# Level 3 cross attention of a Perceiver stack: divisions last, a longer pipeline, the norm in two parts, every second context early

## The chip, the cores and the metric

The kernel runs on one core of one Trainium2 chip. The metric is the device time of one execution in microseconds. The core has five engines with a queue each, and each works its queue strictly in order: PE multiplies matrices (its weight loads are listed as PEld), DVE works on vectors, ACT applies functions, POOL does elementwise work beside them, and SP issues transfers. They wait for each other by semaphores.

## The reference

A stack of four levels updates `x`, 64 batches of 32 rows of width 256. Each level has a cross attention to a context of 64 x 257 rows of width 256, a self attention and a feed-forward part. The change lies in the cross attention of level 3:

```python
qh = _split_heads(q @ Wq.T + bq)      # q = layernorm(x), 32 rows a batch, 16 heads of 16
kh = _split_heads(k @ Wk.T + bk)      # k = v = the batch's context, 257 rows
vh = _split_heads(v @ Wv.T + bv)
score = jnp.einsum('bhqd,bhkd->bhqk', qh, kh) / jnp.sqrt(jnp.float32(D_K))
attn = jax.nn.softmax(score, axis=-1)
out = jnp.einsum('bhqk,bhkd->bhqd', attn, vh)
...
return out @ Wo.T + bo                # added to x
```

Keys and values depend on the context alone, not on `x`, so they can be made at any time before they are needed.

## The kernel before

`x` stays in SBUF as 16 tiles of 128 rows, four batches to a tile (`NB` = 4). The cross attention of level 3 is `l3_xattn`. Its work is cut into steps for a batch b or a tile i:

- `loaded(b)` brings the keys and values of a context that was treated early (tile `kv`, 513 KB, from DRAM), or else its transposed context (tile `cT`, 257 KB).
- `keys_values(b)` does nothing for an early context; for another it makes keys (two halves, evicted by ACT) and values (evicted by DVE) with PE.
- `norm(i)` is the layer norm of a tile: statistics on DVE (L452, L454), the inverse root on POOL (`rsqrt`: L423 adds epsilon into `ln_r_v`, L425 raises it to -1/2 into `ln_r`), and the scaling on DVE (L458). `turned(i)` transposes it, `projected(i)` makes the queries and spreads them over heads (`qb`, POOL, L2713).
- `scores(b)` has PE fill four PSUM tiles `s`, of which there are just four; DVE takes each one's maximum (`nm`, L2788) and ACT its exponential (`e`, L2789) with the sums. The next batch's scores need the tiles back.
- `divided(b)`: DVE inverts the sums (`rs`, L2797), POOL multiplies `e` by them (L2798) and copies the last column (`pc`, L2799).
- `keys_first(b)` turns `e` on PE (L2807) and copies it out in two halves, `eT`, one by DVE (L2811), one by ACT (L2809).
- `weighted(b)` multiplies `eT` with the values; DVE picks each head's own part (`t`, L2825) and sums it into `oT` (L2831).
- `last_rows(i)` carries the weights of the 257th context row through DRAM (`ed`, `es`, SP's queue), and `output(i)` multiplies with the output weights and adds to `x`; POOL adds the bias to `x` (L2732), DVE the product (L2733).

A loop over n from -5 runs one step of each kind a turn, each with its own distance to n: `scores(n)`, `keys_values(n+1)`, `divided(n)`, `weighted(n-2)`, `keys_first(n-1)`; every fourth turn one each of the tile steps. The lists are below in the code and the diff. `as_written` chains the instructions of PE, DVE and ACT in the order in which the loop writes them. POOL's and SP's orders are left to a scheduler when the program is built; once built, they are fixed too.

The early contexts are made by `l3_keys_values`, 16 of them within the feed-forward part of level 0 and 16 within that of level 1, in pieces that `filled` puts between other work of PE there. Before, they are the contexts 0 to 31, so in the loop of `l3_xattn` the first 32 batches have no keys and values to make and the last 32 do.

Of the kernel before, what the change touches and what calls it, by code (L numbers as in the profile page):

```python
# [22 lines left out]
ALU = mybir.AluOpType  # L23
# [3 lines left out]
B, T, S, D = 64, 32, 257, 256  # L27
NT = B * T // 128
NB = 4
KP, KC = 96, 3  # L30
KL = S - 2 * KP
SP = KP * KC
# [2 lines left out]
LN_EPS = 1e-5  # L35
# [288 lines left out]
class Perceiver:  # L324
    def __init__(self, ctx, tc, a):
        self.tc, self.nc, self.a = tc, tc.nc, a
        nc = self.nc
        self.n_tiles = 0
        self.const = ctx.enter_context(tc.tile_pool(name="const", bufs=1))
        self.wpool = ctx.enter_context(tc.tile_pool(name="weights", bufs=N_SLOTS))  # L330
        self.x = self.sb(self.const, [128, NT, D], "x")
        self.cols = self.sb(self.const, [128, N_COL], "cols")
        self.con = self.sb(self.const, [128, N_CON], "con")
        nc.sync.dma_start(self.cols, a["cols"])
        self.ident = self.sb(self.const, [128, 128], "ident")
        make_identity(nc, self.ident)
        self.neg_half = self.sb(self.const, [128, 1], "neg_half")
        nc.gpsimd.memset(self.neg_half, -0.5)
        self.seed = self.sb(self.const, [128, 1], "seed", I32)
        nc.gpsimd.memset(self.seed, RSQRT_SEED + 1)  # L340

        self.ctx_st = self.sb(self.const, [128, 2 * B, 6], "ctx_st")
        self.ctx_st_x = self.sb(self.const, [B, 1, 6], "ctx_st_x")


        self.k_wT = self.sb(self.const, [128, 6, D], "k_wT")
        self.c_mean = self.sb(self.const, [128, B, 2], "c_mean")
        self.c_rc = self.sb(self.const, [128, B, 2], "c_rc")
        self.nxT = self.sb(self.const, [128, 2, B], "nxT")
        dram = ctx.enter_context(tc.tile_pool(name="rows_d", bufs=1, space=bass.MemoryType.DRAM))  # L350
        self.abd = self.sb(dram, [B, 2, S], "abd")

        self.kv = self.sb(dram, [B, 128, 2 * S + 2 * D], "kv")
        self.n_kv = 0

    def forms(self, pool):
# [667 lines left out]
        nc.vector.tensor_tensor(p, lg, bcast(ss, 2, 8), ALU.mult)  # L1024
        return p

    def l3_keys_values(self, one, ps, n):


        nc, a = self.nc, self.a  # L1030
        w = self.sb(one, [128, 2, 2, D], "kv_w")
        for j in range(2):
            nc.sync.dma_start(w[:, j], a["l3x_w"][1 + j].rearrange("p (k n) -> p k n", k=2))
        wk, wv = w[:, 0], w[:, 1]
        todo = range(self.n_kv, self.n_kv + n)
        self.n_kv += n
        ts = {}

        def loaded(b):
            if b in todo:  # L1040
                t = self.sb(self.wpool, [128, 2048], "w")
                nc.sync.dma_start(t[:, 0 : 2 * S], a["ctxT"][b])
                ts[b] = t

        def steps():
            for b in todo[:2]:
                loaded(b)
            for b in todo:
                loaded(b + 2)
                t = ts.pop(b)  # L1050
                cT = t[:, 0 : 2 * S].rearrange("p (k s) -> p k s", k=2)
                kv = t[:, 2 * S : 4 * S + 2 * D]
                for o in range(2):
                    pk = self.sb(ps, [128, S], "h")
                    self.mm(pk, [(wk[:, k, o * 128 : (o + 1) * 128], cT[:, k, :]) for k in range(2)])
                    nc.scalar.activation(
                        kv[:, o * S : (o + 1) * S], pk, AF.Identity, bias=self.col("L3_xattn_bk", o)
                    )
                    yield
                pv = self.sb(ps, [128, 2, D], "y")  # L1060
                for c in range(2):
                    self.mm(pv[:, c, :], [(cT[:, k, c * 128 : (c + 1) * 128], wv[:, k, :]) for k in range(2)])
                    if c == 0:
                        yield
                nc.scalar.copy(kv[:, 2 * S :], pv.rearrange("p c f -> p (c f)"))
                nc.scalar.dma_start(self.kv[b], kv)
                yield

        self.between = steps()

    def filled(self, n=1):
# [80 lines left out]
    def l0_ffn(self):  # L1152
        nc, tc, a = self.nc, self.tc, self.a
        wg = self.weight(a["l0f_wg"], 2)
        with ExitStack() as st:
            one = st.enter_context(tc.tile_pool(name="l0f_1", bufs=1))
            dram = st.enter_context(tc.tile_pool(name="l0f_d", bufs=1, space=bass.MemoryType.DRAM))
            ps = st.enter_context(tc.tile_pool(name="l0f_p", bufs=2, space=PSUM))
            tab = self.routing_tables(one)
            w = self.sb(one, [128, 8, 2048], "w_all")  # L1160
# [5 lines left out]
            rows = st.enter_context(tc.tile_pool(name="l2r", bufs=1))  # L1166
            one1 = st.enter_context(tc.tile_pool(name="l0s", bufs=1))
            pool = st.enter_context(tc.tile_pool(name="l0f", bufs=3))
            self.l3_keys_values(one1, ps, 16)
            p = self.probabilities(one, pool, ps, wg, None, nd)  # L1170
            st.enter_context(self.as_written(nc.vector))
            place = self.places(one, pool, ps, tab, p)
# [30 lines left out]
            at = self.sb(one, [128, NT, 8], "at")  # L1203
# [34 lines left out]
            for s in range(SLOTS):  # L1238
# [23 lines left out]
                y = self.sb(pool, [128, D], "y", bufs=2)  # L1262
# [372 lines left out]
    def l1_ffn(self, ahead, last):  # L1635
# [4 lines left out]
        with ExitStack() as st:  # L1640
# [11 lines left out]
            sums = self.sb(dram, [NT * 128, D], "sums")  # L1652
            nc.scalar.dma_start(sums.rearrange("(i p) f -> p i f", p=128), self.x)
            xn = self.sb(dram, [NT * 128, R], "xn")
            self.l3_keys_values(one, ps, 16)
            p = self.probabilities(one, pool, ps, wr, br, xn)
            nc.scalar.dma_start(xn.rearrange("(i p) f -> p i f", p=128)[:, :, D:R], p)
            place = self.places(one, pool, ps, tab, p)
# [982 lines left out]
    def l3_xattn(self):  # L2641
# [3 lines left out]
        with ExitStack() as st:  # L2645
# [44 lines left out]
                for hh in range(2):  # L2690
                    nc.sync.dma_start(nvd[:, hh::2, :], nv[hh * B : (hh + 1) * B])

            def norm(i):
                t_n[i] = self.normalized(pool, self.x[:, i, :], "n")

            def turned(i):
                pt = self.transposed(ps, t_n[i], "m")
# [48 lines left out]
                    )  # L2746

            def loaded(b):
                kv = self.sb(pool, [128, 2 * S + 2 * D], "kv", bufs=7)
                t_kv[b] = [kv[:, 0 : 2 * S].rearrange("p (k s) -> p k s", k=2), kv[:, 2 * S :].rearrange("p (c f) -> p c f", c=2)]  # L2750
                if b < self.n_kv:
                    nc.sync.dma_start(kv, self.kv[b])
                    return
                cT = self.sb(pool, [128, 2, S], "cT", bufs=4)
                nc.sync.dma_start(cT, a["ctxT"][b].rearrange("p (k s) -> p k s", k=2))
                t_c[b] = cT

            def keys_values(b):
                if b < self.n_kv:
                    return  # L2760
                cT = t_c[b]
                kT, v = t_kv[b]
                for o in range(2):
                    pk = self.sb(ps, [128, S], "m")
                    self.mm(pk, [(wk[:, k, o * 128 : (o + 1) * 128], cT[:, k, :]) for k in range(2)])
                    nc.scalar.activation(kT[:, o, :], pk, AF.Identity, bias=self.col("L3_xattn_bk", o))
                pv = self.sb(ps, [128, 2, D], "m")
                for c in range(2):
                    self.mm(pv[:, c, :], [(cT[:, k, c * 128 : (c + 1) * 128], wv[:, k, :]) for k in range(2)])
                nc.vector.tensor_copy(v, pv)  # L2770

            def scores(b):
                i, bl = b // NB, b % NB
                qb, kT = t_q[i][0], t_kv[b][0]

                pss = [self.sb(ps, [128, S], "s") for _ in range(4)]
                for c in range(2):
                    for r in range(4):
                        f = slice(32 * r, 32 * r + 32)
                        self.mm(  # L2780
                            pss[r][64 * c : 64 * c + 64],
                            [(qb[f, c, bl].rearrange("p h t -> p (h t)"), kT[f, c, :])],
                        )
                nm = self.sb(pool, [128, 4], "nm")
                e = self.sb(pool, [128, 4, S], "e")
                ss = self.sb(pool, [128, 4], "ss")
                for r in range(4):
                    nc.vector.tensor_reduce(nm[:, r : r + 1], pss[r], AX.X, ALU.max, negate=True)  # L2788
                    nc.scalar.activation(  # L2789
                        e[:, r, :], pss[r], AF.Exp, bias=nm[:, r : r + 1], accum_out=ss[:, r : r + 1]  # L2790
                    )
                t_e[b] = e, ss
# [40 lines left out]
                )  # L2833

            st.enter_context(self.as_written(nc.tensor, nc.vector, nc.scalar))
            for n in range(-5, B + 6):

                steps = [(loaded, n + 3, 1), (norm, n + 4, NB), (scores, n, 1), (keys_values, n + 1, 1)]
                steps += [(divided, n, 1), (turned, n + 3, NB), (projected, n + 2, NB)]
                steps += [(weighted, n - 2, 1), (keys_first, n - 1, 1), (last_rows, n - 4, NB), (output, n - 8, NB)]  # L2840
                if n == -4:
                    row_values()
                for step, at, per in steps:
                    if at % per == 0 and 0 <= at < B:
                        step(at // per)
# [95 lines left out]
```

## Time and profile before

Three runs took 3921.47, 3925.65 and 3926.65 us, median 3925.65. The profile is of another execution.

| | |
|---|---|
| profiled execution | 3939.03 us |
| its span | 3937.3 us |
| mean granted clock of TensorE | 0.955 |
| PE busy | 3546.4 us, 90% |
| PE's weight load busy | 2794.3 us, 71% |
| DVE busy | 1963.4 us, 50% |
| ACT busy | 1293.2 us, 33% |
| POOL busy | 1387.9 us, 35% |

The time of an engine is the sum over the whole program; the stages differ much, so a stage has to be read by itself. The granted clock is what the throttle let TensorE have, 1.00 being full speed. Where an engine was idle before an instruction, the profile names the instruction that ended the wait. Instructions are named by line, engine and operation, with the tile written and the tiles read, as `e<-s,nm`.

### The profile page before, as it was taken

To read this page: it belongs to the slowest core of one execution; us is meant where nothing else is said; L and a number is where in the kernel's file an instruction comes from. 1 tells how busy PE (TensorE), PEld (TensorE's weight loads), DVE (VectorE), ACT (ScalarE), POOL (GpSimd) and SP (SyncE) were. 2 spreads that over 40 slices of the span, in tenths; PEclk is the share of its full clock that TensorE was granted. 3 is DMA by queue.
4 is the path that set the end of the run, shared out by engine and by line. 5 is a ranking of instruction groups with operands and counts; after the bars stand their busy time and mean duration, and the time that the engine had idled before them with its cause. 6 is when DMAs were issued, how large, how long until landed. Compare 5 with 4: busy or idle time off the path is not lost.

```text
span 3937.3 us, 74907 instructions
## 1 busy us (share of the span) xinstructions
PE 3546.4 (90%) x29677; PEld 2794.3 (71%) x29677; DVE 1963.4 (50%) x5180; ACT 1293.2 (33%) x3551; POOL 1387.9 (35%) x1752
## 2 busy tenths in 40 slices
PE   7999778879899789799999899979999987998998
PEld 5788446756577667577777566669999965776776
DVE  5555665234344441677766466632222246554454
ACT  2333223423233132333333243322222235543332
POOL 5433751133311113555655244451121135333121
PEclk9999889989999889899999899999999989999999
DMA  6342007256100265333333000010000133110000
GB/s 211 124 153 87 8 7 257 89 188 208 50 2 2 80 184 166 107 91 84 86 85 93 25 1 2 23 66 1 1 1 1 44 102 101 37 42 22 7 7 12
DMA packets 176413, 281.11 MB, mean 71 GB/s; under 512 B 33536, under 2 KB 109824, under 8 KB 171840
## 3 DMA queue, kind: packets, MB, share of 16 engines
q1 hardware_dynamic: 155472, 239.58, 19.7%
q10 hardware_dynamic: 14976, 25.01, 1.8%
q0 software_dynamic: 5616, 11.74, 1.3%
q8 instruction: 236, 3.87, 0.4%
q14 instruction: 113, 0.93, 0.1%
HBM read 243.46 MB, written 32.79 MB: 70 GB/s over the span
## 4 chain that ended last, share of the span: by engine, by line
PE 72%; DVE 11%; POOL 6%; ACT 5%; issue 3%; DMA 2%; ACTq 0%; SPq 0%; DVEq 0%; POOLq 0%
PE m L471 32%; PE p L471 10%; PE s L471 5%; PE y L471 3%; PE h L471 3%; PE b L471 3%; PE o L471 3%; PE ab L471 2%; ACT e L2789 2%; DVE bd L970 2%; PE y L476 2%; PE k L471 1%; PE c L471 1%; POOL e L2798 1%; PE m L465 1%
## 5 line engine op out<-in xcount | busy, mean ns | idle before, releaser
L471 PE MATMUL m<-w,oT 128*128 128x256 f32 x1152 | 272.8, 387 | 23.4 <-ACT eT L2809 15.2
L471 PEld LDWEIGHTS m<-w,oT 128*128 128x128 f32 x1152 | 219.9, 194 | 63.1 <-ACT eT L2809 17.0
L471 PE MATMUL m<-nTg,w 128*128 128x256 f32 x1024 | 234.7, 387 | 4.3 <-ACT k L1520 2.9
L471 PEld LDWEIGHTS m<-nTg,w 128*128 128x128 f32 x1024 | 193.3, 192 | 35.6 <-ACT k L1520 4.9
L2798 POOL TENSOR_TENSOR e<-e,rs 128x1028 f32<-128x1028 f32 x64 | 121.7, 1902 | 200.2 <-DVE rs L2797 200.2
L471 PE MATMUL s<-cT,ut 128*128 128x257 f32 x768 | 181.1, 386 | 0.0
L471 PE MATMUL m<-pT,cn 128*128 128x384 f32 x512 | 176.2, 487 | 2.5 <-DVE pT L2174 2.5
L2151 ACT ACTIVATE p<-s,bi 128x257 f32<-128x257 f32 x192 | 88.9, 472 | 247.0 <-DVE bi L2147 226.7
L423 POOL TENSOR_SCALAR ln_r_v<-ln_mv 128x1 f32<-128x1 f32 x176 | 38.7, 223 | 348.1 <-DVE ln_mv L454 266.3
L471 PEld LDWEIGHTS s<-cT,ut 128*128 128x128 f32 x768 | 143.5, 193 | 19.4 <-ACT p L2151 0.2
L2789 ACT ACTIVATE e<-s,nm 128x257 f32<-128x257 f32 x256 | 118.1, 474 | 113.4 <-DVE nm L2788 93.1
L970 DVE STREAM_TRANSPOSE bd<-hs_p 32x512 f32<-32x512 f32 x192 | 134.8, 702 | 40.2 <-POOL hs_p L964 37.0
L2120 POOL TENSOR_TENSOR cT<-cT,ab 128x514 f32<-128x514 f32 x64 | 82.4, 1288 | 205.4 <-PE m L471 85.8
L471 PEld LDWEIGHTS m<-pT,cn 128*128 128x128 f32 x512 | 96.5, 189 | 58.7 <-DVE pT L2174 2.9
L2255 POOL TENSOR_TENSOR sr<-ss,neg_half 128x16 f32<-128x16 f32 (+1 forms) x33 | 95.0, 2879 | 113.1 <-DVE ss L2253 113.1
L471 PE MATMUL m<-w,nT 128*128 128x512 f32 (+2 forms) x320 | 126.2, 536 | 8.8 <-ACT nT L829 8.2
L2545 POOL TENSOR_TENSOR tB<-hB 128x512 f32<-128x512 f32 x8 | 10.2, 1271 | 326.2 <-ACT hB L2583 326.2
L471 PE MATMUL ab<-nTg,w 128*128 128x256 f32 x512 | 117.1, 388 | 6.5 <-DVE hA L2561 5.5
L471 PE MATMUL m<-w,nTg 128*128 128x512 f32 x256 | 117.7, 604 | 0.0
L471 PEld LDWEIGHTS ab<-nTg,w 128*128 128x128 f32 x512 | 98.2, 194 | 23.3 <-DVE hA L2561 9.2
L2160 POOL TENSOR_TENSOR p<-p,rs 128x771 f32<-128x771 f32 x64 | 95.2, 1488 | 46.7 <-DVE rs L2159 27.9
L471 PE MATMUL o<-bd,v 128*64 128x128 f32 (+1 forms) x1536 | 90.1, 287 | 21.4 <-DVE bd L970 21.4
(712 smaller groups left out, 8819.9 us busy)
## 6 DMA issues: line engine op xcount, KB each, us to landing
ct<-in_ctx SPq DMA_DIRECT2D x192, 256.0 KB
cT<-in_ctxT SPq DMA_DIRECT2D x32, 1028.0 KB
cT<-in_ctxT SPq DMA_DIRECT2D x96, 257.0 KB
ab<-abd SPq DMA_DIRECT2D x64, 257.0 KB
kv<-w ACTq DMA_DIRECT2D x32, 513.0 KB
kv<-kv SPq DMA_DIRECT2D x32, 513.0 KB
rb<-rd SPq DMA_DIRECT2D x16, 514.0 KB
w<-in_ctxT SPq DMA_DIRECT2D x32, 257.0 KB
```

Source lines behind the costliest of these rows:

```text
L423: nc.gpsimd.tensor_scalar(t, src, eps, None, ALU.add)
L465: self.nc.tensor.transpose(out[:, c, :], src[:, c * 128 : (c + 1) * 128], self.ident)
L471: self.nc.tensor.matmul(out, lhsT=l, rhs=r, start=j == 0, stop=j == last)
L476: self.nc.tensor.matmul(out[:, 0:n], lhsT=cT[0], rhs=self.k_qm[:, 0, 0:n], start=True, stop=False)
L970: self.nc.vector.transpose(bd[q, :, b, :], p[q])
L2120: nc.gpsimd.tensor_tensor(cT, cT, bcast(ab[:, 0, :], 1, 2), ALU.mult)
L2151: nc.scalar.activation(p[:, g, :], pss[g], AF.Exp, bias=bi[:, g : g + 1], accum_out=ss[:, g : g + 1])
L2160: nc.gpsimd.tensor_tensor(p, p, bcast(rs, 2, S), ALU.mult)
L2255: nc.gpsimd.tensor_tensor(r, ss, self.neg_half[:p].to_broadcast([p, nh]), ALU.pow)
L2545: nc.gpsimd.tensor_tensor(t1, b12, b11, ALU.subtract)
L2789: nc.scalar.activation(e[:, r, :], pss[r], AF.Exp, bias=nm[:, r : r + 1], accum_out=ss[:, r : r + 1])
L2798: nc.gpsimd.tensor_tensor(e, e, bcast(rs, 2, S), ALU.mult)
```

## The change

- `divided(n)`, so far behind the keys and values in a turn, comes after `weighted`, `keys_first` and the first part of the norm. `weighted` works on n-3 instead of n-2 and `keys_first` on n-2 instead of n-1; `last_rows` and `output` follow one turn later. There are four tiles `e` instead of three and eight tiles `kv` instead of seven.
- `norm` is cut into `norm_1` (statistics and POOL's inverse root) and `norm_2` (the scaling), a turn apart. The order of a turn begins with `norm_2`, ahead of `scores`; `norm_1` stands ahead of `divided`.
- The early contexts are every second one, 1, 3, ... 63 (`early`), instead of 0 to 31. The PSUM tiles of `l3_keys_values` come from a function that is passed in, with 512 columns each.

```diff
+EARLY = 32
...
+        self.early = [b for b in range(B) if (b + 1) * EARLY // B > b * EARLY // B]
...
-    def l3_keys_values(self, one, ps, n):
+    def l3_keys_values(self, one, n, bank, buf=None):
...
-        todo = range(self.n_kv, self.n_kv + n)
+        todo = self.early[self.n_kv : self.n_kv + n]
...
-                    pk = self.sb(ps, [128, S], "h")
+                    pk = bank(o)[:, 0:S]
...
-                pv = self.sb(ps, [128, 2, D], "y")
+                pv = bank(2)
...
-            self.l3_keys_values(one1, ps, 16)
+            self.l3_keys_values(one1, 16, lambda j: self.sb(ps, [128, 512], "hhy"[j]))
...
-            self.l3_keys_values(one, ps, 16)
+            self.l3_keys_values(one, 16, lambda j: self.sb(ps, [128, 512], "hhy"[j]))
...
-            def norm(i):
-                t_n[i] = self.normalized(pool, self.x[:, i, :], "n")
+            def norm_1(i):
+                st = self.sb(pool, [128, 6], "ln_st")
+                nc.vector.bn_stats(st, self.x[:, i, :])
+                mv = self.sb(pool, [128, 2], "ln_mv")
+                nc.vector.bn_aggr(mv, st)
+                t_n[i] = mv, self.rsqrt(pool, mv[:, 1:2], LN_EPS, "ln_r")
+
+            def norm_2(i):
+                mv, r = t_n[i]
+                t_n[i] = self.sb(pool, [128, D], "n")
+                nc.vector.tensor_scalar(t_n[i], self.x[:, i, :], mv[:, 0:1], r, ALU.subtract, ALU.mult)
...
-                kv = self.sb(pool, [128, 2 * S + 2 * D], "kv", bufs=7)
+                kv = self.sb(pool, [128, 2 * S + 2 * D], "kv", bufs=8)
...
-                if b < self.n_kv:
+                if b in self.early:
...
-                e = self.sb(pool, [128, 4, S], "e")
+                e = self.sb(pool, [128, 4, S], "e", bufs=4)
...
-            for n in range(-5, B + 6):
-
-                steps = [(loaded, n + 3, 1), (norm, n + 4, NB), (scores, n, 1), (keys_values, n + 1, 1)]
-                steps += [(divided, n, 1), (turned, n + 3, NB), (projected, n + 2, NB)]
-                steps += [(weighted, n - 2, 1), (keys_first, n - 1, 1), (last_rows, n - 4, NB), (output, n - 8, NB)]
+            for n in range(-6, B + 8):
+
+                steps = [(loaded, n + 3, 1), (norm_2, n + 4, NB), (scores, n, 1), (keys_values, n + 1, 1)]
+                steps += [(turned, n + 3, NB), (projected, n + 2, NB), (weighted, n - 3, 1)]
+                steps += [(keys_first, n - 2, 1), (norm_1, n + 5, NB), (divided, n, 1), (last_rows, n - 5, NB), (output, n - 9, NB)]
```

More of the change, by code (lines that the diff above doesn't have):

```diff
@@ L1039, in loaded @@
         def loaded(b):
[L1040 to L1043, printed above, removed]
+            t = buf() if buf else self.sb(self.wpool, [128, 2048], "w")
+            nc.sync.dma_start(t[:, 0 : 2 * S], a["ctxT"][b])
+            ts[b] = t
         def steps():
@@ L1047, in steps @@
                 loaded(b)
-            for b in todo:
-                loaded(b + 2)
+            for at, b in enumerate(todo):
+                for c in todo[at + 2 : at + 3]:
+                    loaded(c)
                 t = ts.pop(b)
@@ L1059, in steps @@
                     yield
-                pv = self.sb(ps, [128, 2, D], "y")
+                pv = bank(2)
                 for c in range(2):
-                    self.mm(pv[:, c, :], [(cT[:, k, c * 128 : (c + 1) * 128], wv[:, k, :]) for k in range(2)])
+                    self.mm(
+                        pv[:, c * D : (c + 1) * D],
+                        [(cT[:, k, c * 128 : (c + 1) * 128], wv[:, k, :]) for k in range(2)],
+                    )
                     if c == 0:
                         yield
-                nc.scalar.copy(kv[:, 2 * S :], pv.rearrange("p c f -> p (c f)"))
+                nc.scalar.copy(kv[:, 2 * S :], pv)
                 nc.scalar.dma_start(self.kv[b], kv)
@@ L2758, in keys_values @@
             def keys_values(b):
-                if b < self.n_kv:
+                if b in self.early:
                     return
```

## The prediction

> **What bounds the kernel now.** I read the share of busy time by engine first (PE 90%), then stretches of the cross attention of level 3, which runs from the end of the first scores (3201.4 us) to the last output (3593.15 us), 391.7 us. Columns: stretch and its length, busy time of PE, PE's weight load, DVE, ACT and POOL with counts, granted TensorE clock, DMA share, GB/s.
>
> ```profile
> 3201.40:3370.00 168.60, 134.89 (x1438) 96.61 (x1442) 109.79 (x292) 88.98 (x332) 89.55 (x106) 0.93 0.31 95
> 3370.00:3593.20 223.20, 218.35 (x1892) 172.07 (x1886) 130.93 (x315) 108.86 (x369) 81.48 (x94) 1.00 0.14 40
> ```
>
> The first stretch holds the contexts whose keys and values were made early: PE idles there and the clock is 0.93. The second makes keys and values itself and PE is full. So interleaving the two kinds can fill the idle time, if the order of the waits allows it. The timeline of PE in the second stretch gives each piece of work at full clock (start, duration, instruction):
>
> ```profile
> 3454.55 0.69 PE L471 MATMUL s<-kv,qb 32*64 32x257 f32 x16
> 3455.16 2.00 PE L471 MATMUL m<-cT,w 128*128 128x257 f32 x8
> 3457.01 1.89 PE L471 MATMUL m<-w,cT 128*128 128x256 f32 x8
> ...
> 3459.04 1.14 PE L471 MATMUL m<-eT,kv 128*64 128x128 f32 x16
> 3460.12 1.09 PE L2807 MATMUL m<-ident,e 128*128 128x128 f32 x8
> ```
>
> From start to start: scores 0.62, keys and values 3.63, weighting 1.07, turning of e 1.02; once in four steps also 0.31 (turned), 0.98 (projected) and 1.49 (last rows and output). Four steps without keys and values are 4x2.71 + 2.79 = 13.63 us of PE, with them 28.15 (measured 28.24, so nothing is lost there). The early groups of four begin their outputs at 3242.01, 3263.15, 3284.36, 3304.05, 3325.31 and 3345.01: 20.60 each, 6.97 lost. All PE work is 64x2.71 + 32x3.63 + 16x2.79 = 334.2; the stage loses 57.5: 8 early groups 55.8, 8 late ones 0.7, edges 1.0.
>
> Where an early group loses it: DVE's, POOL's and PE's timelines over the same few microseconds (in brackets: idle time before, and what ended it).
>
> ```profile
> 3298.50 0.68 DVE L2811 COPY eT<-m 128x512 f32<-128x512 f32 x1
> 3299.09 0.42 DVE L452 BATCH_NORM_STATS2 ln_st<-x 128x6 f32<-128x256 f32 x1
> 3299.55 0.18 DVE L454 BATCH_NORM_AGGREGATE ln_mv<-ln_st 128x2 f32<-128x6 f32 x1
> 3300.74 0.41 DVE L458 TENSOR_SCALAR n<-x,ln_mv,ln_r 128x256 f32<-128x256 f32 x1 [1.02 <-POOL ln_r L425]
> ```
>
> ```profile
> 3297.72 1.90 POOL L2798 TENSOR_TENSOR e<-e,rs 128x1028 f32<-128x1028 f32 x1 [1.03 <-DVE rs L2797]
> 3299.68 0.19 POOL L2799 COPY pc<-e 128x4 f32<-128x4 f32 x1
> 3299.84 0.22 POOL L423 TENSOR_SCALAR ln_r_v<-ln_mv 128x1 f32<-128x1 f32 x1
> 3300.14 0.57 POOL L425 TENSOR_TENSOR ln_r<-ln_r_v,neg_half 128x1 f32<-128x1 f32 x1
> ```
>
> ```profile
> 3300.31 1.09 PE L2807 MATMUL m<-ident,e 128*128 128x128 f32 x8
> 3301.24 0.27 PE L2738 MATMUL m<-ident,pc 128*16 128x128 f32 x1
> 3304.05 2.07 PE L471 MATMUL m<-w,oT 128*128 128x256 f32 x4 [2.54 <-ACT eT L2809]
> 3305.92 1.06 PE L471 MATMUL m<-nvs,es 128*128 128x256 f32 x2
> ```
>
> DVE waits 1.02 for the norm's root from POOL, its queue stands, and PE idles 2.54. Then PE's work takes twice its time (2.07 against 1.03 in the late half). Stretches of 1 us of PE (busy, count, clock, DMA share, GB/s) say why:
>
> ```profile
> 3304.00:3305.00 1.00, 0.95 (x2) 0.50 0.01 3
> 3305.00:3306.00 1.00, 1.00 (x4) 0.50 0.02 5
> 3306.00:3307.00 1.00, 1.00 (x11) 0.50 0.00 0
> ```
>
> The clock is halved for about 3.4 us. Of the five such gaps listed, three were followed by this (groups of 21.14, 21.21, 21.26 us), two not (19.69, 19.70): 1.5 us each time.
>
> **The change, part by part.** *Every second context early.* As many contexts, matmuls, evictions and loads as before, here and in the two earlier stages that make them; PSUM tiles of 512 columns take the turns of those of 257 and 2x256. Cost there 0. Here odd steps n now do keys and values (of the even context n+1), even steps do not. A group of four needs 13.63 + 2x3.63 = 20.89 of PE.
>
> *Loads.* A pair brings 513 + 257 KB in some 13 us, 59 GB/s, against 95 carried in the first stretch without PE once waiting for a kv load. SP's queue holds the last rows' ed and es issues (four es take 1.7 us) ahead of loads needed about five steps, over 25 us, later; 0.
>
> *Divisions last, turning and weighting a step later.* DVE no longer stands for the exponentials (rs waits 1.1 us in each early step): t, oT and the copy eT come first, and rs finds its sums ready. The fourth e tile and eighth kv tile cover the extra step. On POOL the two qb (0.56 each) now stand ahead of the division of step 2 mod 4, and x + bo (0.72, after norm_2) ahead of that of step 0; a division is needed by PE two steps later, over 10 us, so 0. This gain is inside the PE-bound sum.
>
> *The norm in two parts.* This decides. norm_1 (statistics) stands on DVE at the end of a step n = 3 mod 4, ahead of rs; norm_2 stands first in the next step, ahead of the maxima nm. The built order of POOL in the changed kernel is ln_r_v, then e (the division of that step), then ln_r, then pc. So ln_r stands behind 1.90 us of division, DVE's queue behind norm_2, the exponentials behind nm, and the next scores behind the exponentials, which hold the four s banks. And the step is even: no keys and values cover it.
>
> I work it out from durations above, t = 0 at the start of scores(3). PE: scores to 0.62, keys and values to 4.25, weighting to 5.32, turning to 6.34, scores(4) to 6.96. DVE: t and oT 5.37 to 6.35, eT to 6.95, statistics to 7.5, rs to 7.7. POOL: ln_r_v at 7.7, e 7.9 to 9.8, ln_r to 10.35. DVE: norm_2 10.4 to 10.7, then nm at 0.33 each; the first exponential starts 0.53 after the first nm (11.25), they follow at 0.45; a bank is free 0.47 + 0.14 later (at the stage's start PE restarted 0.14 after an exponential): 11.85 for the first, 13.2 for the fourth, so scores(5) end at 13.6. Meanwhile weighting starts 0.15 late, as eT's two copies are not done, and turning ends at 9.2; without the wait scores(5) would end at 9.8. The group loses 3.80 + 0.15 = 3.95. The other three steps lose nothing: odd ones have keys and values, step 2 mod 4 has projected (0.98) on top of 2.09, against some 2.5 for nm and exponentials.
>
> That happens at n = 0, 4, ... 56: 15x3.95 = 59.3. Step 60 has no norm; its chain of nm and exponentials alone loses 0.85. Edges 1.0 as before. At the start the first norm's statistics run ahead of the row values while DVE waits for a DMA, which takes about 1.7 off, and keys and values of context 0 come in (3.63, partly under the 1.2 of qb): first scores end 0.6 earlier (bounds -0.8 and, at half clock, +3). Loss after: 59.3 + 0.85 + 1.0 - 0.6 = 60.5, against 57.5: +3.0 us before the clock is counted.
>
> *The clock.* The new gap is 9.2 to 11.85, 2.65 us, and then 1.4 us of scores that trickle in as banks come free. No row shows this very gap. Nearest: the 2.54 us gap, which halved the clock in 3 of 5 groups. Lower bound c = 0, as in the other two. Upper bound 3.3: at the stage's start the clock read 0.50 from 3198.25 to 3211.5, four spells in a row, with PE working between gaps; two spells cost 3.3. I take one spell in every group, since the low stretch is 4 us instead of 2.54: half of 3.4 us with keys and values queued behind, 1.7. 15x1.7 = 25.5.
>
> [...]
>
> Sum: +3.0 + 25.5 = +28.5. The profiled execution took 3939.03 (span 3937.3), 13.4 above the median of the three runs, 3925.65; on its span I expect 3966, on the median 3954. The runs spread over 5 us; 0.2% (7.9 us) is about what can be told from no change.
>
> **Rivals.**
> *Faster: the root comes in time.* If ln_r did not stand behind the division, or DVE reached norm_2 late, only the chain of nm and exponentials would be left, 0.85 a group: 15x0.85 + 0.85 + 1.0 - 0.6 = 14.0 of loss, -43.5, 3882. For it: PE has 57.5 to give and no other engine is above 66% in either stretch. Against it: POOL's and DVE's orders as built. With the clock staying full it decides from a loss of 3.75 a group; with c = 1.7, from 2.05.
>
> *The clock stays full.* c = 0 to 0.3: +3 to +7.5, 3929 to 3933. For it: two of five gaps. Against it: the trickle, which leaves PE nearly idle for longer.
>
> *Two spells a group.* c = 2.5 to 3.3: +40 to +52, 3966 to 3978. For it: the start of the stage, where sparse work did not bring the clock back; against it: in the groups of before one spell was always enough.
>
> *The gain does not appear because loads are late*: a kv load 3 us late in each group would add 45. I see nothing for it and fold it into the case above.
>
> **How the numbers follow.** Forecast (c 0.4 to 2.4: 3935 to 3965) 0.58; clock full 0.13; two spells 0.13; root in time 0.16. Predicted 3954. The range leaves out the last rival and the far end: from 3922 (+3 less an error of 0.4 a group) to 3975. Faster by over 0.2%: 0.16 less a little, 0.15. Within 0.2%: most of the full clock, 0.10. Slower: 0.75.
>
> **What would show it.** Right: DVE's n waits about 2.7 us for ln_r in 15 places, POOL shows e between ln_r_v and ln_r, ACT's exponentials wait for nm at every fourth step, PE idles 2.6 us there with 0.50 clock after it, groups of 26 to 27 us; rs no longer waits for exponentials. Wrong: n hardly waits, groups near 22, or the clock at 1.00 throughout the stage and groups near 24.8.

## The result, and the profile after

| | before | after |
|---|---|---|
| median of the runs | 3926.15 us (3921.47 to 3931.77, 4 runs) | 3970.55 us (3966.25 to 3971.83, 4 runs) |
| profiled execution, its span | 3939.03, 3937.3 | 3966.25, 3964.5 |
| cross attention of level 3, first scores' end to last output's end | 391.7 | 427.3 (3193.96 to 3621.25) |
| PE work of that stage at full clock | 334.2 | 334.2 |
| a group of four batches | 20.60 early, 28.24 late | 24.9 to 27.5 |

The change makes the kernel slower: ratio 1.0104, 95% interval 1.0089 to 1.0119. Groups are measured here between PE's starts of the projection of one tile and the next.

The stage grew by 35.6 us. The two halves no longer differ, and the clock is 0.91 in both. Stretches of the stage, columns as in the prediction (busy time of PE, PE's weight load, DVE, ACT and POOL with counts, granted clock, DMA share, GB/s):

```profile
3194.00:3400.00 206.00, 184.64 (x1566) 137.14 (x1568) 113.18 (x291) 98.84 (x348) 85.36 (x102) 0.91 0.23 68
3400.00:3621.30 221.30, 197.75 (x1741) 147.86 (x1738) 126.29 (x320) 100.60 (x351) 88.38 (x105) 0.91 0.19 57
```

The place itself, a turn n = 0 mod 4, in the timelines of DVE, POOL and PE (start, duration, instruction, idle time before and what ended it):

```profile
3402.59 0.18 DVE L2704 BATCH_NORM_AGGREGATE ln_mv<-ln_st 128x2 f32<-128x6 f32 x1
3402.69 0.16 DVE L2813 RECIPROCAL rs<-ss 128x4 f32<-128x4 f32 x1
3405.51 0.41 DVE L2710 TENSOR_SCALAR n<-x,ln_mv,ln_r 128x256 f32<-128x256 f32 x1 [2.66 <-POOL ln_r L428]
3405.84 1.41 DVE L2804 TENSOR_REDUCE nm<-s 128x1 f32<-128x257 f32 x4
```

```profile
3402.86 0.22 POOL L426 TENSOR_SCALAR ln_r_v<-ln_mv 128x1 f32<-128x1 f32 x1 [4.63 <-DVE rs L2813]
3403.05 1.90 POOL L2814 TENSOR_TENSOR e<-e,rs 128x1028 f32<-128x1028 f32 x1
3404.90 0.57 POOL L428 TENSOR_TENSOR ln_r<-ln_r_v,neg_half 128x1 f32<-128x1 f32 x1
```

```profile
3403.35 1.09 PE L2823 MATMUL m<-ident,e 128*128 128x128 f32 x8
3406.97 2.52 PE L474 MATMUL s<-kv,qb 32*64 32x257 f32 x16 [2.52 <-ACT e L2805]
3409.41 3.80 PE L474 MATMUL m<-cT,w 128*128 128x257 f32 x8
```

POOL has both values it needs at 3402.9. It takes the division `e` between the two halves of the root, so `ln_r` starts 2.04 us after `ln_r_v` instead of 0.3. DVE stands 2.66 us in front of `n` with four maxima behind it, and PE idles 2.52 us until the first exponential frees a bank. Then the next keys take 3.80 us where a matmul group of that kind took 2.00 in the late half before. Single microseconds of PE over the same place (busy, count, clock, DMA share, GB/s):

```profile
3406.00:3407.00 1.00, 0.03 (x1) 0.67 0.00 0
3407.00:3408.00 1.00, 1.00 (x5) 0.50 0.00 0
...
3412.00:3413.00 1.00, 1.00 (x3) 0.50 0.00 0
3413.00:3414.00 1.00, 1.00 (x6) 0.91 0.06 16
```

The clock is halved from 3406.35 to 3413.2: 6.8 us, twice the spell of about 3.4 that the kernel before showed. Over the whole stage, the waits of DVE and of PE (total us, times, longest):

```profile
DVE n L2710 <- POOL ln_r L428: 38.2, 15, 2.7
...
DVE rs L2813 <- ACT e L2805: 1.3, 2, 1.0
```

```profile
PE s L474 <- ACT e L2805: 38.3, 15, 3.1
```

The wait that the change was to remove is gone: `rs` waited 35.0 us in 32 places for the exponentials before, 1.3 now. In its place `n` waits 38.2 in 15 places (14.1 in 14 before), and PE's wait for the exponentials is of the same size and number. In 14 of the 15 places `n` waits 2.66 us behind the division. The first, at the stage's start, is another case: no division stands there yet, `n` waits 1.00 for the root alone, and PE's 3.06 are the length of the chain from the norm's statistics to the first exponential.

### The profile page after: what moved, and what is told of

It reads as the page before. It is cut to its first block, busy times and chain, and to the rows that moved or that the text cites. A ratio compares the mean times of both kernels' runs of the same rounds, so it can differ in the third digit from the quotient of the medians.

```text
span 3964.5 us, 74957 instructions
## 1 busy us (share of the span) xinstructions
PE 3571.5 (90%) x29677; PEld 2807.0 (71%) x29677; DVE 1962.4 (50%) x5180; ACT 1295.6 (33%) x3551; POOL 1386.9 (35%) x1752
## 3 DMA queue, kind: packets, MB, share of 16 engines
q1 hardware_dynamic: 155472, 239.58, 19.6%
## 4 chain that ended last, share of the span: by engine, by line
PE 73%; DVE 11%; POOL 5%; issue 4%; ACT 4%; DMA 3%; ACTq 0%; SPq 0%; DVEq 0%; POOLq 0%
PE m L474 33%; PE p L474 10%; PE s L474 6%; PE b L474 3%; PE y L474 3%; PE o L474 3%; PE h L474 3%; PE ab L474 2%; PE y L479 1%; DVE bd L973 1%; PE c L474 1%; PE k L474 1%; PE m L468 1%; PE m L2823 1%; PE y L480 1%
```

## The experiments

Theory: the built order of POOL, division ahead of `ln_r`, costs 3.95 us a group in a turn that no keys and values cover, and the clock falls in that gap. Rivals: the norm being in two parts is itself the trouble; the place of `norm_2` on DVE is; the clock is a minor part; interleaving the early contexts costs by itself (PSUM turns, loads). Each kernel was timed against the kernel before. Its stage and its group come from its profiled execution:

| kernel | median us | ratio [95%] | stage us | group us |
|---|---|---|---|---|
| before | 3926 to 3930 | | 391.7 | 20.6 early, 28.24 late |
| after | 3970.55 | 1.0104 [1.0089, 1.0119] | 427.3 | 27.31, at first 24.9 to 26.7 |
| norm_1 ahead of the division | 3895.51 | 0.9918 [0.9901, 0.9934] | 351.1 | 21.71 |
| norm whole again | 3976.05 | 1.0117 [1.0101, 1.0134] | 427.5 | 27.31 |
| norm_2 behind the maxima | 3902.66 | 0.9936 [0.9919, 0.9952] | 360.8 | 22.56 |
| the gap filled with matmuls | 3949.23 | 1.0057 [1.004, 1.0075] | 404.2 | 25.55 |
| even contexts early | 3918.15 | 0.997 [0.9958, 0.9982] | 379.4 | 23.61 |
| contexts 0 to 31 early | 3941.85 | 1.0032 [1.0019, 1.0044] | 408.6 | 19.6 to 20.6, then 29.95 to 31.7 |
| before, contexts interleaved | 3930.04 | 0.9999 [0.9988, 1.0009] | 385.7 | 23.88 |
| norm_1 ahead, output a turn earlier | 3879.65 | 0.9868 [0.9845, 0.9891] | 340.5 | 21.07 |

**The statistics moved ahead of the division.** The step `norm_1` is issued behind the maxima of the same turn, so that POOL meets the root before the division:

```diff
-steps = [(loaded, n + 3, 1), (norm_2, n + 4, NB), (scores, n, 1), (keys_values, n + 1, 1)]
+steps = [(loaded, n + 3, 1), (norm_2, n + 4, NB), (scores, n, 1), (norm_1, n + 5, NB), (keys_values, n + 1, 1)]
...
-steps += [(keys_first, n - 2, 1), (norm_1, n + 5, NB), (divided, n, 1), (last_rows, n - 5, NB), (output, n - 9, NB)]
+steps += [(keys_first, n - 2, 1), (divided, n, 1), (last_rows, n - 5, NB), (output, n - 9, NB)]
```

> The changed kernel with norm_1 moved up in the turn, right behind scores, and nothing else; in the built order of POOL ln_r then stands ahead of the division instead of behind it. Theory (the root stands behind 1.90 us of division, and DVE's queue with it): n no longer waits, the maxima start about 3 us earlier in 15 turns, scores end 0.65 late instead of 3.8, the clock stays full: groups of four near 21.7 us instead of 27.2, about 82 us less, near 3889. Rival (the longer pipeline, the later divisions or the interleaving cost the time, the norm's place is incidental): 3960 or more.

Measured: 3895.51 us, stage 351.1, group 21.71. POOL's and DVE's timelines of this kernel at the same turn:

```profile
3402.47 0.22 POOL L426 TENSOR_SCALAR ln_r_v<-ln_mv 128x1 f32<-128x1 f32 x1
3402.77 0.57 POOL L428 TENSOR_TENSOR ln_r<-ln_r_v,neg_half 128x1 f32<-128x1 f32 x1
3406.66 1.98 POOL L2814 TENSOR_TENSOR e<-e,rs 128x1028 f32<-128x1028 f32 x1 [3.32 <-DVE rs L2813]
```

```profile
3406.41 0.17 DVE L2813 RECIPROCAL rs<-ss 128x4 f32<-128x4 f32 x1
3406.49 0.39 DVE L2710 TENSOR_SCALAR n<-x,ln_mv,ln_r 128x256 f32<-128x256 f32 x1
```

The root is done 3.1 us before DVE reaches `n`, which has no wait any more, although the division is still issued at the same place. The stage falls by 76.2 us. This kernel holds everything else of the change, interleaving, longer pipeline, two-part norm, so that the place of `norm_1` alone turns a slower kernel into a faster one. The edit brings the statistics forward on DVE as well as the root on POOL; what the order on POOL does with the statistics left where they were, no run shows by itself.

**The norm in one piece again**, at the first place of the turn:

```diff
+def norm(i):
+    norm_1(i)
+    norm_2(i)
...
-steps = [(loaded, n + 3, 1), (norm_2, n + 4, NB), ...
+steps = [(loaded, n + 3, 1), (norm, n + 4, NB), ...
-steps += [(keys_first, n - 2, 1), (norm_1, n + 5, NB), (divided, n, 1), ...
+steps += [(keys_first, n - 2, 1), (divided, n, 1), ...
```

> The changed kernel with the norm in one part again at the head of the turn, as in the kernel before; divisions stay last, so in POOL's built order the division still stands ahead of the root. Theory (what costs is the division ahead of the root, not the cut in two): n still waits over 2 us, the maxima start only 0.35 us earlier; 5 us less, with the clock perhaps up to 20 less: 3950 to 3966. Rival (the cut of the norm costs the time): n waits 1.0 us as in the kernel before, 50 us or more less, 3920 or below.

Measured: 3976.05 us, stage 427.5, group 27.31. POOL's and DVE's timelines of this kernel:

```profile
3409.97 1.90 POOL L2818 TENSOR_TENSOR e<-e,rs 128x1028 f32<-128x1028 f32 x1 [4.16 <-DVE rs L2817]
3411.84 0.22 POOL L426 TENSOR_SCALAR ln_r_v<-ln_mv 128x1 f32<-128x1 f32 x1
...
3412.15 0.57 POOL L428 TENSOR_TENSOR ln_r<-ln_r_v,neg_half 128x1 f32<-128x1 f32 x1
```

```profile
3412.75 0.41 DVE L2714 TENSOR_SCALAR n<-x,ln_mv,ln_r 128x256 f32<-128x256 f32 x1 [2.33 <-POOL ln_r L428]
```

The cut of the norm is not the cause. Whole, the norm has both halves of the root behind the division, and DVE stands 2.33 us instead of 2.66. PE's gap is 2.18 instead of 2.52, and 13 of these 14 gaps were followed by two spells of half clock. That the wait is slightly shorter brought nothing: both kernels come out with groups of 27.31. The expectation, 3950 to 3966, missed. That the clock took back what the shorter wait gave is read from the equal groups, not tested.

**norm_2 behind the maxima**, with `norm_1` where the change put it:

```diff
-steps = [(loaded, n + 3, 1), (norm_2, n + 4, NB), (scores, n, 1), (keys_values, n + 1, 1)]
+steps = [(loaded, n + 3, 1), (scores, n, 1), (norm_2, n + 4, NB), (keys_values, n + 1, 1)]
```

> The changed kernel with norm_2 one place later in the turn, behind scores, so that DVE takes the maxima first; POOL's order stays (division ahead of the root). Theory (the wait is costly only because the maxima are queued behind it): n still waits, 1 to 2 us in 15 places, but exponentials and scores go on; about 80 us less, 3887 to 3897. Rival (a late root is costly wherever it stands): less than 20 us gained, 3950 or more.

Measured: 3902.66 us, stage 360.8, group 22.56. DVE's waits of this kernel:

```profile
DVE n L2710 <- POOL ln_r L428: 18.9, 14, 1.4
```

DVE still waits behind the division, for 1.4 us in 14 places, but the maxima have gone ahead and PE's next scores don't depend on the wait. The time fell by 68 us of the 75 that the first experiment gave, somewhat less than expected. So most of what the wait costs is set by what is queued behind it on DVE.

**The gap filled.** The after kernel, with matmuls on constant operands put at the end of each turn n = 0 to 56, n = 0 mod 4, where PE would idle. They go into a PSUM tile of which only one column is read, by a copy of ACT:

```diff
+def filler(n):
+    if n < 0 or n > 56:
+        return
+    pf = self.sb(ps, [128, 2, 128], "m")
+    for j in range(10):
+        self.mm(pf[:, j % 2, :], [(wq[:, k, 0:128], wq[:, k, 128:256]) for k in range(2)])
+    f = self.sb(pool, [128, 1], "filler")
+    nc.scalar.copy(f, pf[:, 1, 0:1])
...
+                if n % NB == 0:
+                    filler(n)
```

> The changed kernel with 20 extra matmuls of 128x128x128 (about 2.5 us of PE) at the end of every fourth turn, in the place of PE's gap; their result is thrown away (one column copied by ACT). The wait itself stays. Theory (half clock after the gap costs 1.7 to 3.4 us in each of 15 groups): the clock stays at 1.00, groups fall from 27.2 to 24.9, 30 to 36 us less, 3935 to 3941. Rival (the clock is incidental, all of the loss is the wait): no change, 3970, or more if the extra matmuls cost time.

Measured: 3949.23 us, stage 404.2, group 25.55. A long stretch and PE's timeline of this kernel:

```profile
3200.00:3400.00 200.00, 199.12 (x1955) 162.82 (x1955) 116.86 (x297) 98.59 (x353) 85.68 (x104) 1.00 0.23 65
```

```profile
3410.52 4.63 PE L474 MATMUL m<-w 128*128 128x128 f32 x40
3415.08 0.69 PE L474 MATMUL s<-kv,qb 32*64 32x257 f32 x16
```

The clock is 1.00 throughout, and the stage is 23.1 us shorter with 68 us more of PE work in it. The filler was mis-sized: 20 matmuls came out as 40 records and 4.63 us, not the 2.5 that I meant. The scores behind it start 4.56 us after the filler's start, where gap and trickle of the after kernel are 2.52 and 2.04 - 0.62 = 1.42, together 3.94; so it overshoots by about 0.6 in each of 15 groups, 9 us. The clock's part of the loss is then about 23.1 + 9 = 32 us, as an estimate. That is nearly all of the 35.6 by which the stage grew. It holds for the profiled execution, which was the fastest of the four (3937.34; the others 3945 to 3954); between the medians of the two kernels the gain is 21.3.

**The even contexts early** instead of the odd ones, everything else as in the after kernel. The wait stays and its turn now has keys and values:

```diff
-self.early = [b for b in range(B) if (b + 1) * EARLY // B > b * EARLY // B]
+self.early = list(range(0, B, 2))
```

> The changed kernel with the even contexts early (0, 2, ... 62) instead of the odd ones, and nothing else. The order of POOL stays (division ahead of the root), but the turn in which norm_2 waits now has keys and values to make, and the uncovered turn before it has none. Theory (the wait costs what no matmul work covers): n waits as long as in the changed kernel, but PE stands only about 1.45 us there (until the keys' eviction, which ACT does after the exponentials) and 0.85 in the turn before; groups near 23.3 us, no half clock; 60 us less than the changed kernel, 3905 to 3920. Rival (the wait is a fixed price wherever it falls): 3960 or more.

Measured: 3918.15 us, stage 379.4, group 23.61. DVE's and PE's waits in this kernel:

```profile
DVE n L2710 <- POOL ln_r L428: 38.4, 15, 2.7
```

```profile
PE m L2823 <- ACT kv L2782: 22.7, 14, 1.6
```

DVE's wait is as before the edit, 38.4 us in 15 places, and the kernel is 52 us faster. What remains is a smaller gap of 1.6 us: the eviction of keys stands behind the late exponentials on ACT, and PE's turning has to wait for it. After these gaps the clock stayed at 1.00. Here the parity of the early contexts alone decides whether the wait is covered.

**The first 32 contexts early**, as before the change, with the rest of the change:

```diff
-self.early = [b for b in range(B) if (b + 1) * EARLY // B > b * EARLY // B]
+self.early = list(range(EARLY))
```

> The changed kernel with the contexts 0 to 31 early, as in the kernel before: the new order without the interleaving. Theory: in the first half every turn is uncovered, groups stay near 20 us (norm's wait and half clock in place of the old waits); in the second half keys and values cover all but 1.5 to 2 us of the wait, groups 30 instead of 28.24: 3930 to 3950, between the kernel before and the changed one. Rival (the new order alone is the loss, the interleaving does not matter): 3965 or more.

Measured: 3941.85 us, stage 408.6. The early half of the stage takes 19.6 to 20.6 a group, the late half 29.95 to 31.7 against 28.24 of pure PE work. In the early half the wait of `n` lies uncovered and the clock falls at each of its seven gaps (2.09 to 2.52 us), as in the after kernel, though without keys and values the group is short. In the late half keys and values cover the wait itself, but seven gaps of 1.88 us before PE's turning stay, as in the experiment before, on top of 28.24 of PE work; four of them were followed by a half clock of some 3.4 us. Against the after kernel this is 29 us less: with half of the waits covered and half not, the kernel lies between the two.

**The kernel before, with the odd contexts early and nothing else** (the loop that loads ahead in `l3_keys_values` is fitted to a list; the PSUM tiles stay as before):

```diff
+self.early = list(range(1, B, 2))
...
-todo = range(self.n_kv, self.n_kv + n)
+todo = self.early[self.n_kv : self.n_kv + n]
...
-if b < self.n_kv:
+if b in self.early:
```

> The kernel before with every second context early and nothing else. Theory: without the later divisions an uncovered turn still takes some 4.1 us of DVE and ACT (the chain of maxima, exponentials, inverse sums, t, oT, eT in the profile of before) against 2.71 of PE, and the norm's turn 6 to 7: groups of 23.6 to 25 us, against 24.4 on the mean of the kernel before, so 3915 to 3945, little changed. Rival (interleaving by itself fills PE): 3890 or below.

Measured: 3930.04 us, stage 385.7, group 23.88. DVE's waits of this kernel:

```profile
DVE rs L2798 <- ACT e L2790: 35.7, 33, 1.2
```

Interleaving by itself changes nothing that can be told in the median (0.9988 to 1.0009) and takes 6 us off the stage. The wait of `rs` for the exponentials is untouched by it. So the loads of the interleaved contexts cost nothing that shows. The PSUM tiles of 512 columns are not in this kernel, but the profiles bear on them: the time outside the stage is 3545.5 and 3549.1 us in the two kernels with the old tiles and 3531.3 to 3548.0 in the eight with the new ones, so no cost of theirs stands out of that spread. Interleaving without the rest of the change does not bring the gain; which part of the rest it needs was not separated.

PE idles here too, 13 times for 2.52 to 2.53 us ahead of the output, and only the first of these gaps was followed by a half clock. The last section comes back to this.

**The first experiment, with the output a turn earlier.** Of its group of 21.71 PE's own work is 20.89. The output is issued in turn n = 1 mod 4, a turn that has keys and values as well; this edit puts it in the turn before, which has none:

```diff
-steps += [(keys_first, n - 2, 1), (divided, n, 1), (last_rows, n - 5, NB), (output, n - 9, NB)]
+steps += [(keys_first, n - 2, 1), (divided, n, 1), (last_rows, n - 5, NB), (output, n - 8, NB)]
```

> The changed kernel with norm_1 right behind scores and output one turn earlier (n - 8), so that its 1.49 us of PE stand in the turn n = 0 mod 4, whose matmuls are too short for the chain of maxima and exponentials. Theory: the last 0.8 us of a group (21.71 against 20.89 of PE) falls to 0.1 or 0.2: 9 to 10 us less than with norm_1 moved alone, about 3886. Rival (what is left of the 0.8 is not that chain): no change, 3895.

Measured: 3879.65 us, stage 340.5, group 21.07. The stage fell by 10.6 us, as expected, and the median by 15.9. The two profiled executions differ by 11.05 (3891.95 and 3880.90), nearly all of it the stage; where the rest of the difference of the medians lies is open. A stretch of this kernel:

```profile
3197.20:3400.00 202.80, 200.55 (x1969) 154.26 (x1970) 141.68 (x366) 122.27 (x435) 107.38 (x127) 1.00 0.29 86
```

PE is busy 200.55 of 202.80 us at full clock. The stage is within 6.3 us of its PE work of 334.2. This kernel is 1.3% faster than the kernel before and 2.3% faster than the changed one.

## Why the prediction was right

Forecast 3954 us with a range of 3922 to 3975; measured 3970.55, slower by 1.0%. Taken by the steps of the prediction:

- **The stall.** This step held in 14 of its 15 places: the built order of POOL, `n` waiting 2.66 us (2.7 worked out), maxima, exponentials and scores queued behind, a gap of 2.52 (2.65) and a trickle. The first place, n = 0, was counted with the others but has no division ahead of the root; its gap of 3.06 is of a like size by luck. The one group that kept the full clock throughout, the last with a norm, took 25.02 (24.84 worked out: 20.89 + 3.95). That the late root is the cause is shown by the first experiment, that the place in DVE's queue matters by the third, and that the missing cover matters by the fifth.
- **Divisions last, at a gain within the PE-bound sum.** Held: `rs` waits 1.3 us instead of 35.0. With the stall out of the way the rest of the change, of which this is a part, is worth more than interleaving alone: 385.7 with interleaving alone, 351.1 with all of the change and the root in time.
- **Zero for interleaving, PSUM turns and loads.** Held as far as it shows: 0.9999 for interleaving alone, no time outside the stage that stands out with the new PSUM tiles, and no wait of an engine within the stage that a kv load ended.
- **The start, -0.6.** From the last addition of level 2 to the end of the first scores took 20.8 us before and 20.1 after: -0.7.
- **The clock: the term that was mis-sized.** I took one spell of 3.4 us a group, 1.7 us, 25.5 in all. Of the 15 gaps 14 were followed by a half clock, five by one spell of 3.41 us and nine by spells of 6.83. Against the 25.02 of the group at full clock, the three full groups with one spell lost 1.6 each and the nine with two lost 2.33 each: 4.8 + 21.0. The two first gaps, in groups that have no output yet, add some 1.7 each by half the length of their spells (an estimate), so about 29 in all; the filled gap gave about 32. The argument that failed is "in the groups of before one spell was always enough". It weighed gaps that were followed by dense work. Here the scores that follow come in as banks come free. The better row for a second spell was the one used for the upper bound, the stage's start, though its 3.3 is more than the 2.33 that two spells cost here.

The sum for the stage: 334.2 + 86.6 worked out, the start aside, against 427.3, 6.5 short. The clock's 3.5 and the 0.18 of the group at full clock, taken in 15 places, account for it within 1 us, although what the first and last turns cost is not separated in that.

The step from stage to total was not as good. The stage grew by 35.6, less 0.7 for the start; the medians differ by 44.4 over four runs each, or about 40 against the 25 runs of before in the later comparisons. The profiled execution of before was 13 us above its median, and the earlier levels of that of after took 6.8 us less than in that of before; so those two profiles can't be compared outside the stage. Five to nine us of the difference between the medians are not accounted for. What the experiments say of the stage does not rest on them.

Two agreements are therefore luck or of little weight. The span of 3966 worked out for a profiled execution came out at 3964.5 because the 6.5 by which the stage was underrated and the 6.8 of the earlier levels cancel. And the median lies in the band of the rival "two spells a group" (3966 to 3978), above the forecast's own (3935 to 3965), only by the time that is not accounted for: the 34.9 of stage and start, added to the median of before, give 3961. Of the mechanism that rival was right for nine groups of fifteen, at 2.33 each and not 2.5 to 3.3.

The rival "the clock stays full" (3929 to 3933) was wrong: of the 15 gaps, 14 of 2.52 us and one of 3.06, 14 were followed by a half clock. Gaps of 2.52 us could cost clock here, and so could 2.18 with the whole norm (13 of 14) and 1.88 with the contexts 0 to 31 early (four of seven), while 14 of 1.62 with the even contexts early did not. But the length does not decide it by itself: of the 13 gaps of 2.52 to 2.53 in the kernel before with contexts interleaved 12 kept the full clock.

The first rival, "the root comes in time" (3882), was wrong for this kernel and close for the first experiment, which is just that: 3895.51. Its stage loses 351.1 - 334.2 = 16.9, against 14.6 worked out for the rival, the start aside.

## What to carry to other kernels

Read the built order of every queue for a short operation that has come behind a long one, here 0.57 us behind 1.90 on a helper engine, and then ask what is queued behind the operation that waits for it. The same wait of 2.7 us cost 76 us of a stage in one turn and, by the same comparison with the first experiment, 28 us (379.4 against 351.1) in a turn where other matmuls covered part of it. Where a gap on PE can't be avoided, count the clock after it as well: here 14 of 15 gaps of 2.52 to 3.06 us were followed by a half clock, nine of them for two spells of 3.41 us, with scores trickling in behind each.

## What was not expected of the hardware

- **Half clock for two spells.** The nine long spells began 0.3 to 0.7 us before the scores after the gap started, the five short ones 1.0 to 2.5 us after. The other kernels with trickling scores fall in line: 13 long spells with the whole norm began with the scores (0.02 us after), and with the contexts 0 to 31 early the long ones began at most 0.7 after, the short ones 1.6 and 2.5. In the first case the scores that trickle in, with idle PE ahead of them, fall into the first spell, and a second follows; in the other dense keys and values fall into it. That this is the reason fits the records and was not tested by a run of its own.
- **Where the gap lies between the spells.** In every trace here the half-clock spells in and around the stage last 3.41 us or a multiple, and within a kernel they start a multiple of 3.41 us apart (in the changed kernel the first and the last of the nine long ones start at 3324.43 and 3542.88, 64 times 3.413 apart). Stretches of 3.41 us, laid end to end through the spells on record, sort gaps of one length. PE in these stretches at the first two gaps of the kernel before with contexts interleaved (busy time of PE with count, clock, DMA share, GB/s):

```profile
3247.48:3250.89 3.41, 1.34 (x13) 1.00 0.00 0
3250.89:3254.30 3.41, 2.96 (x14) 0.50 0.03 7
...
3271.37:3274.78 3.41, 2.60 (x41) 1.00 0.00 0
3274.78:3278.20 3.42, 1.60 (x14) 1.00 0.01 2
```

The first gap of 2.53 us has 2.08 in one stretch, and the next stretch ran at half clock; the second is cut into 0.71 and 1.81 and did not cost clock, nor did the 11 behind it, cut alike. It is the same with the gaps of 2.54 in the kernel before, of which the prediction left open why three of five halved the clock: four of all six have 2.33 to 2.54 in one stretch and were followed by a half clock, the two with 1.6 were not. At 1.86 to 1.89 of 3.41 both happened: in the changed kernel three gaps with 1.86 in one stretch were followed by a half clock and the last, with 1.86 too, was not; with the contexts 0 to 31 early four with 1.88 or 1.89 were and one with 1.88 was not. Where scores trickle in behind the gap, their waits seem to count too: in the changed kernel two stretches with only 0.87 and 0.89 of the gap were followed by a half clock. No kernel was built that moves a gap and nothing else, so this is read from the records.
- **Groups that lock.** From the sixth gap on the groups of the changed kernel are 27.30 to 27.35 us long with one of 27.40 and a first of 27.49, and the kernel with the whole norm, whose wait is 0.33 us shorter, has the same 27.31. In both kernels the long spells of one group and the next start 27.31 us apart, eight times 3.41. A group that would take 25.02 and loses time by the clock seems to settle at a length at which its gap lies at the same place between the spells: in the changed kernel the part of the gap ahead of the spell's start was 2.23, 2.05, 1.95, 1.91, 1.88, 1.87 and then three times 1.86 us, with the whole norm all 2.18 of it in each of the 13 places. This is read from the records, not tested. The last gap of the changed kernel, at the same place (1.86) by this count, was not followed by a half clock, so the place is not the whole of it.
- **Records of matmuls.** The filler's 20 matmuls of 128x128x128 in fp32 were 40 records and 4.63 us, 0.23 us for each one issued.
